# Layer 2 of a twelve-sublayer network on one core: FP4 magnitudes in PSUM, other slots, and kept queue order in the stage before

## The chip, the core and the metric

The kernel runs on one core of a Trainium2 chip (trn2). The metric is the device time of one launch in microseconds (us), lower is better. A core has five engines with a queue each, worked off in the order in which they were built: PE (matrix products and transposes, with its weight loads shown as PEld), DVE (vector), ACT (scalar functions), POOL (GpSimd) and SP (here only DMA issues).

## The reference, cut to what matters

The input is `x` of shape 8 x 512 x 128 in fp32, eight sequences, called batches b here. Twelve sublayers follow each other, each on a layernorm of `x`, each added to `x`. The parts that this case is about:

```python
# layer 1, twice: routed experts with a shared expert (stage l1_ffn), between them 16-head attention (stage l1_attn)
x = x + 0.5 * _L1_ffn_ref(_layernorm(x), ...)
x = x + _L1_attn_ref(_layernorm(x), ...)
x = x + 0.5 * _L1_ffn_ref(_layernorm(x), ...)
# layer 2 and the first sublayer of layer 3 (one stage, layer2)
x = x + 0.5 * _L2_ffn_ref(_layernorm(x), ...)      # FFN with FP4 rounding
x = x + _L2_attn_ref(_layernorm(x), ...)           # gated recurrence along the 512 tokens
x = x + 0.5 * _L2_ffn_ref(_layernorm(x), ...)
x = x + 0.5 * _L3_ffn_ref(_layernorm(x), ...)      # relu FFN
...
def fp4_quant_dequant(x):                          # blocks of 16 along the last axis
    scale = max(max(abs(x)) / 6, 1e-12)
    q = _GRID[searchsorted(_MID, abs(x / scale))] * sign(x) * scale
def _L2_ffn_ref(x, w_gate, w_up, w_down):          # 128 -> 352 -> 128
    h = silu(fp4(x) @ fp4(w_gate).T) * (fp4(x) @ fp4(w_up).T)
    return fp4(h) @ fp4(w_down).T
```

## The kernel before, in words

All eight batches of `x` stay in SBUF for the whole launch. The stages run one after the other: l0_ffn, l0_attn, l0_ffn, l1_ffn, l1_attn, l1_ffn, layer2, l3_attn, l3_ffn. A list scheduler takes the instructions in the order of the program as priorities and pulls an instruction forward where its own clock says that the engine is free and the operands are there; so the order in an engine's queue is not the order of the program. `in_order` (L366) chains the instructions of the named engines that are traced inside its block, so that they keep their order; each block is a chain of its own.

**Stage l1_attn.** For each batch, PE makes scores into PSUM tiles `first` (three banks), DVE takes their row maxima (`max`, L1590, 64 per batch), ACT takes exponentials, PE multiplies with the values. At the end of a batch, `attended` updates `x` on POOL (L1771).

**Stage l1_ffn.** For each batch, `routed(b + 1)` (norm, router, ranks, shares) is emitted in steps between the ten steps of `experts(b)`. An expert is two products (`pg`, `pu`), a silu on ACT (L913), two DVE products (L914, L922) and a product into `po`. In its second run the stage also carries, in the steps (b, 3) and (b, 8), pieces of `layer2_constants`: the decay rate of the recurrence by a chain of small DVE operations (`softplus`), and the FP4 rounding of the three layer-2 weights. The norm in `routed` is `norm` (L322 to L338): eight small DVE instructions, two on POOL, four more on DVE. Before the change no block of this second run is chained, since `aside_at` has an empty set of engines.

**Stage layer2.** Each of the four sublayers is cut into pieces for one batch (or for a pair of batches in the recurrence), each piece has a slot, and all pieces are sorted by slot and emitted in that order. The slot of a piece is that of `_ROUNDED_FFN`, `_RECURRENCE` or `_RELU_FFN`, plus `_STARTS[k]`, plus `_STEPS[k]` times b, with k = 0 for the first FP4 FFN, 1 for the recurrence, 2 for the second FP4 FFN, 3 for the relu FFN.

The pieces of an FP4 FFN for one batch: `stats` and `apply` (norm, the multiplication on ACT), `x_in` and `x_out` (rounding of the normed input), `turned` (transposes on PE, copy on ACT), four `gated` (per 128 tokens: `pg` and `pu` on PE, silu on ACT L1182, product on DVE L1183), `h_in` and `h_out` for two halves (rounding of 704 columns), `h_turned` for two halves (three times two transposes into `ht` L1198 and a copy on ACT L1199), `down` (twelve products into `po`, added to `x` on DVE L431).

Rounding is `fp4_in` (DVE: maximum, scale, reciprocal, L1015 to L1025; then POOL multiplies, L1027) and `fp4_out`: ACT writes `big` = |r| times 2^22 (L1035), DVE passes twice over `big` and `r` (L1036, L1037), POOL multiplies by the scale (L1038). `big` is an SBUF tile with two buffers; `r` lies in SBUF.

PSUM has eight banks in this stage: `mm` two, `pg` two, `pu` two, `ht` one, `po` one.

Of the kernel before, what the change touches and what calls it, by code (L numbers as in the profile page):

```python
# [19 lines left out]
F32 = mybir.dt.float32  # L20
# [6 lines left out]
P = 128  # L27
NB, L, D = 8, 512, 128
NC = L // P
# [173 lines left out]
def _attention_pack(p, wq, bq, wk, bk, wv, bv, wo, bo):  # L203
# [17 lines left out]
    sums=(9, 14, 21, 29),  # L221
    turned=(17, 23, 29, 35),
# [18 lines left out]


_STARTS = (0, 7, 32, 40)
_STEPS = (5.5, 8, 8, 8)
_DOWN = [(0, 128), (128, 128), (256, 96)]
_ROUNDED_FFN = {
    "stats": -9,
    "apply": -5,
    "x_in": -5,
    "x_out": -4,  # L250
    "turned": -1.5,
    "gated": (0.5, 0.5, 1, 1),
    "h_in": (0.5, 2.5),
    "h_out": (2, 4),
    "h_turned": (3.5, 5),
    "down": 7,
}
_RECURRENCE = {
    "stats": -1,
    "apply": 2,  # L260
    "turned": 2,
    "gates": 3.5,
    "decays": 4,
    "exps": 4,
    "roots": 4.5,
    "sums": 5.5,
    "added": 6.5,
}
_RELU_FFN = {
    "stats": 0.5,  # L270
    "apply": 0.5,
    "turned": 2,
    "wide": (3.5, 3.5, 4, 4),
    "product": 5.5,
    "added": 10,
}


class _Kernel:
# [554 lines left out]
    def l1_ffn(self):  # L834


        nc, tc = self.nc, self.tc
        with ExitStack() as s:
            keep = s.enter_context(tc.tile_pool(name="keep", bufs=1))
            self.sb = s.enter_context(tc.tile_pool(name="sb", bufs=2))  # L840
            self.ps = s.enter_context(tc.tile_pool(name="ps", bufs=2, space=bass.MemoryType.PSUM))
            self.shares = keep.tile([P, 8, P], F32R, name="shares")
            nc.vector.tensor_copy(
                self.shares.rearrange("p e m -> p (e m)"), self.w["moe", "spread"]
            )
            self.seqs = [{} for _ in range(NB)]
            for _ in self.routed(0):
                pass
            for b in range(NB):
                ahead = self.routed(b + 1) if b + 1 < NB else iter(())  # L850
                experts = self.experts(b)
                ordered = self.aside_at[0] if b == 1 else ()
                for step in range(10):
                    with self.in_order(*ordered):
                        next(experts)
                        next(ahead, None)
                        if (b, step) in self.aside_at[1]:
                            next(self.aside, None)
                for _ in ahead:
                    pass  # L860
# [166 lines left out]
        nc.gpsimd.tensor_tensor(self.blocks(r), self.blocks(v), self.each(inv), ALU.mult)  # L1027
        return r, scale

    def fp4_out(self, r, scale, sb):  # L1030


        nc = self.nc
        big = sb.tile([P, 2 * 352], F32, name="big")[:, : r.shape[1]]
        nc.scalar.activation(big, r, AF.Abs, scale=2.0**22)  # L1035
        nc.vector.scalar_tensor_tensor(r, big, 1.5 * 2.0**22, r, ALU.max, ALU.add)  # L1036
        nc.vector.scalar_tensor_tensor(r, big, 1.5 * 2.0**22, r, ALU.max, ALU.subtract)  # L1037
        nc.gpsimd.tensor_tensor(self.blocks(r), self.blocks(r), self.each(scale), ALU.mult)  # L1038
# [116 lines left out]
    def rounded_ffn(self, b):  # L1155
        nc = self.nc
        F = 352
        flat = "p c d -> p (c d)"
        wT = self.l2w
        stats, apply, q = self.front(b, "f", 3)  # L1160

        def x_in():
            q["x"] = self.fp4_in(q["xn"].rearrange(flat), self.sb, "x", 3)

        def x_out():
            self.fp4_out(*q["x"], self.sb)

        def turned():
            q["xT"] = self.sb.tile([P, L], F32, name="fxT", bufs=3)
            xq = q["x"][0].rearrange("p (c d) -> p c d", d=D)  # L1170
            self.transposed(xq, self.ps, q["xT"], nc.scalar.copy)

        def gated(c):
            if c % 2 == 0:
                q["h", c // 2] = self.sb.tile([P, 2, F], F32, name="h", bufs=3)
            h = q["h", c // 2][:, c % 2, :]
            tok = q["xT"][:, bass.ts(c, P)]
            pg = self.ps.tile([P, L], F32, name="pg")[:, :F]
            self.mm(pg, tok, wT["w_gate"])
            pu = self.ps.tile([P, L], F32, name="pu")[:, :F]  # L1180
            self.mm(pu, tok, wT["w_up"])
            nc.scalar.activation(h, pg, AF.Silu)  # L1182
            nc.vector.tensor_tensor(h, h, pu, ALU.mult)  # L1183

        def h_in(half):
            q["r", half] = self.fp4_in(q["h", half].rearrange(flat), self.sb, "h", 3)

        def h_out(half):
            self.fp4_out(*q["r", half], self.sb)

        def h_turned(half):
            if half == 0:
                q["hT"] = self.sb.tile([P, 3, L], F32, name="hT", bufs=2)
            hq = q["r", half][0].rearrange("p (j f) -> p j f", f=F)
            for k, (at, n) in enumerate(_DOWN):
                pt = self.ps.tile([P, 2, P], F32, name="ht", bufs=1)
                for j in range(2):
                    nc.tensor.transpose(pt[:n, j, :], hq[:, j, at : at + n], self.ident)  # L1198
                nc.scalar.copy(  # L1199
                    q["hT"][:n, k, bass.ts(half, 2 * P)], pt[:n].rearrange("p c t -> p (c t)")  # L1200
                )

        def down():
            po = self.ps.tile([P, L], F32, name="po", bufs=1)
            for c in range(NC):
                for k, (_, n) in enumerate(_DOWN):
                    self.mm(
                        po[:, bass.ts(c, P)],
                        q["hT"][:n, k, bass.ts(c, P)],
                        wT["w_down"][:n, k, :],  # L1210
                        start=k == 0,
                        stop=k == 2,
                    )
            self.add_half(b, po.rearrange("p (c d) -> p c d", d=D))

        s = _ROUNDED_FFN
        return [
            (s["stats"], stats),
            (s["apply"], apply),
            (s["x_in"], x_in),  # L1220
            (s["x_out"], x_out),
            (s["turned"], turned),
            *((s["gated"][c], partial(gated, c)) for c in range(4)),
            *((s["h_in"][k], partial(h_in, k)) for k in range(2)),
            *((s["h_out"][k], partial(h_out, k)) for k in range(2)),
            *((s["h_turned"][k], partial(h_turned, k)) for k in range(2)),
            (s["down"], down),
        ]

    def recurrence(self, bs):  # L1230
# [7 lines left out]
        sb = self.sb  # L1238
# [10 lines left out]
        def gates():  # L1249
            for k, (_, _, _, q) in enumerate(qs):  # L1250
                for n, bank in (("ig", "pg"), ("ag", "pu")):
                    pg = self.ps.tile([P, L], F32, name=bank)
                    self.mm(pg, a(n + "_w"), q["xT"])
                    q[n] = make(n, k)
                    nc.scalar.activation(q[n], pg, AF.Sigmoid, bias=a(n + "_b"))
# [31 lines left out]
        def added():  # L1287
# [8 lines left out]
            (s["stats"], lambda: all_of(1)),  # L1296
            (s["apply"], lambda: all_of(2)),
            *((s[f.__name__], f) for f in (turned, gates, decays, exps, roots, sums, added)),
        ]

    def relu_ffn(self, b):
        nc = self.nc
        w = lambda n: self.w["l3f", n]
        stats, apply, q = self.front(b, "r", 1)
# [4 lines left out]
            q["h"] = self.sb.tile([P, 4, L], F32, name="rh", bufs=1)  # L1309

        def wide(k):
            ph = self.ps.tile([P, L], F32, name=("pg", "pu")[k % 2])
            self.mm(ph, w("w1")[:, bass.ts(k, P)], q["xT"])
            nc.scalar.activation(q["h"][:, k, :], ph, AF.Relu, bias=w("b1")[:, k : k + 1])

# [7 lines left out]
        def added():  # L1323
# [8 lines left out]
            (s["apply"], apply),  # L1332
            (s["turned"], turned),
            *((s["wide"][k], partial(wide, k)) for k in range(4)),
            (s["product"], product),
            (s["added"], added),
# [468 lines left out]
@with_exitstack  # L1805
def _run_stages(ctx, tc, u, packs, out):
    k = _Kernel(ctx, tc, u, packs, out)
    for at, name in enumerate(_STAGES):
        if at == 3:
            k.aside = k.attention_constants(ctx)  # L1810
            next(k.aside)
            k.aside_at = (mybir.EngineType.Pool, mybir.EngineType.DVE), [(1, n) for n in range(10)]
        if at == 5:
            k.aside = k.layer2_constants(ctx)
            next(k.aside)
            k.aside_at = (), [(b, n) for b in range(NB - 1) for n in (3, 8)]
        getattr(k, name)()
    k.store()

# [17 lines left out]
```

## Time and profile before

| | us |
|---|---|
| median of three runs | 2488.74 (2488.4 to 2490.4) |
| profiled execution, its own time | 2481.17 |
| its span, first to last instruction | 2479.4 |
| stage l1_attn in the trace | about 750 to 1272 |
| second l1_ffn in the trace | about 1272 to 1529 |
| layer2 in the trace | 1529 to 1946 |
| busy in the span: PE, DVE, ACT, POOL | 2147.4, 1657.7, 1235.7, 671.0 |

A row of the timeline is: start, duration, engine, line and operation, output and inputs; in brackets the idle time of that engine just before it, and the instruction of another engine that ended it. A row of the groups is: line, engine, operation, shapes and count; then busy time in us and mean ns of one; then the idle time before and what ended it. A row of the windows is a stretch of the span, its length, and the busy time (and the number of instructions) of each engine in it, then the share of full speed granted to PE, the share of the DMA engines, and GB/s.

### The profile page before, as it was taken

The numbers are of one execution on the slowest core, as the hardware profiler recorded it, in microseconds if no ns is written. First come the engines' busy times: TensorE is split into PE (matmuls) and PEld (weight loads), VectorE is DVE, ScalarE is ACT, GpSimd is POOL, SyncE is SP. The second block draws the span as 40 slices with busy tenths as digits, with TensorE's granted clock in tenths as the row PEclk, the third lists the DMA queues.
The fourth block names the chain that finished last, engine by engine and source line by source line (L and its number), as shares of the span: only waits on it lengthen the run. The fifth ranks groups of instructions, "written<-read, shape, count | busy, mean of one in ns | idle before, by whom it ended". The sixth has DMA issues, their size and how long they took to land.

```text
span 2479.4 us, 30103 instructions
## 1 busy us (share of the span) xinstructions
PE 2147.4 (87%) x10907; PEld 1031.0 (42%) x10967; DVE 1657.7 (67%) x3830; ACT 1235.7 (50%) x1828; POOL 671.0 (27%) x923
## 2 busy tenths in 40 slices
PE   7679998889998989888869997776778899999989
PEld 3444444434444333333324443544444444444444
DVE  4566774568768788888547776879677465666611
ACT  3545663323321667667633333556655235555554
POOL 1123443022111011111121112556555013333330
PEclk9779998989996899999979998878889879999999
DMA  3000000000000000000000000000000000000001
GB/s 118 1 1 1 1 1 13 10 0 1 0 1 0 1 1 1 1 1 1 1 7 1 0 1 0 1 1 1 0 1 1 0 1 1 1 1 1 1 1 34
DMA packets 10036, 13.08 MB, mean 5 GB/s; under 512 B 416, under 2 KB 8736, under 8 KB 9760
## 3 DMA queue, kind: packets, MB, share of 16 engines
q1 hardware_dynamic: 7776, 10.11, 1.2%
q8 instruction: 86, 1.41, 0.2%
q10 hardware_dynamic: 2112, 1.05, 0.2%
q14 instruction: 62, 0.51, 0.1%
HBM read 9.06 MB, written 2.10 MB: 5 GB/s over the span
## 4 chain that ended last, share of the span: by engine, by line
PE 61%; DVE 20%; POOL 9%; ACT 6%; issue 4%; DMA 0%; ACTq 0%; DVEq 0%; SPq 0%; POOLq 0%
PE pair L312 10%; PE av L312 8%; PE first L312 7%; PE po L312 7%; PE mm L312 6%; PE pg L312 5%; PE pu L312 5%; DVE max L1590 4%; ACT e L1698 2%; PE ck L312 2%; PE pr L312 1%; PE pw L312 1%; PE ph L312 1%; PE pi L312 1%; PE pf L312 1%
## 5 line engine op out<-in xcount | busy, mean ns | idle before, releaser
L1590 DVE TENSOR_REDUCE max<-first 128x1 f32<-128x512 f32 (+3 forms) x864 | 534.1, 663 | 189.1 <-PE first L312 165.8
L1698 ACT ACTIVATE e<-pair 128x1024 f32<-128x1024 f32 (+3 forms) x512 | 436.4, 865 | 251.4 <-PE pair L312 239.0
L312 PE MATMUL first<-qkT 32*128 32x512 f32 (+3 forms) x1024 | 341.1, 473 | 40.7 <-DVE max L1590 39.4
L312 PE MATMUL av<-e,v 128*32 128x512 f32 (+3 forms) x2048 | 239.7, 538 | 1.0
L312 PE MATMUL pair<-qkT 32*128 32x512 f32 (+3 forms) x1024 | 223.6, 455 | 19.6 <-ACT e L1698 13.1
L913 ACT ACTIVATE act<-pg 128x512 f32<-128x512 f32 x144 | 86.0, 597 | 233.4 <-PE pg L312 198.4
L312 PEld LDWEIGHTS first<-qkT 32*128 32x128 f32 x1024 | 154.4, 198 | 107.9 <-DVE max L1590 99.1
L312 PE MATMUL pair<-mT,max_rows 32*128 32x512 f32 (+3 forms) x1024 | 192.6, 378 | 1.8 <-DVE mT L1632 1.8
L312 PEld LDWEIGHTS pair<-qkT 32*128 32x128 f32 x1024 | 95.7, 186 | 233.5 <-ACT e L1698 130.8
L1700 POOL TENSOR_SCALAR_AFFINE_SELECT e<-e 128x256 f32<-128x256 f32 x256 | 103.4, 407 | 252.9 <-ACT e L1698 252.5
L312 PE MATMUL po<-act,w_moe 128*128 128x512 f32 x288 | 156.7, 630 | 2.4 <-DVE act L922 2.1
L312 PE MATMUL pg<-xT,w_moe 128*128 128x512 f32 x288 | 153.6, 616 | 0.0
L312 PE MATMUL pu<-xT,w_moe 128*128 128x512 f32 x288 | 148.7, 599 | 0.0
L914 DVE TENSOR_TENSOR act<-act,pu 128x512 f32<-128x512 f32 x144 | 98.2, 682 | 55.7 <-PE pu L312 53.7
L1596 POOL COPY copies<-max 128x128 f32<-128x128 f32 x64 | 22.6, 410 | 337.8 <-DVE max L1590 337.8
L312 PEld LDWEIGHTS pair<-mT,max_rows 32*128 32x128 f32 x1024 | 97.2, 189 | 3.6 <-DVE mT L1632 3.3
L922 DVE TENSOR_TENSOR act<-act,pw 128x512 f32<-128x512 f32 x128 | 87.0, 681 | 15.6 <-PE pw L312 13.8
L951 POOL TENSOR_TENSOR ge<-ge,w_moe 128x64 f32<-128x64 f32 (+1 forms) x32 | 42.8, 1336 | 193.9 <-DVE ge L949 191.0
L1198 PE MATMUL ht<-w_const,h_r 128*128 128x128 f32 (+1 forms) x192 | 47.8, 339 | 53.6 <-POOL h_r L1038 29.4
L1557 ACT CAST qkT<-pair 128x1024 fp32r<-128x1024 f32 x64 | 64.7, 1013 | 41.2 <-PE pair L312 40.7
L312 PEld LDWEIGHTS pu<-xT,w_moe 128*128 128x128 f32 x288 | 53.6, 192 | 63.8 <-issue 59.0
L421 PE MATMUL mm<-w_const,xn 128*128 128x128 f32 x192 | 39.7, 323 | 41.7 <-DVE xn L338 26.0
(398 smaller groups left out, 4299.4 us busy)
## 6 DMA issues: line engine op xcount, KB each, us to landing
w_moe<-in_moe SPq DMA_DIRECT2D x1, 2392.0 KB, 14.2
out<-x SPq DMA_DIRECT2D x8, 256.0 KB, 2.3
x<-in_u ACTq DMA_DIRECT2D x4, 256.0 KB, 6.6
x<-in_u SPq DMA_DIRECT2D x4, 256.0 KB, 6.5
w_mixer<-in_l0a SPq DMA_DIRECT2D x1, 960.5 KB, 8.2
w_mixer<-in_l1a SPq DMA_DIRECT2D x1, 769.0 KB, 4.3
w_ffn<-in_l0f SPq DMA_DIRECT2D x1, 578.0 KB, 7.3
w_ffn<-in_l2f SPq DMA_DIRECT2D x1, 560.0 KB, 3.3
```

Of the source, the lines that this page charges most:

```text
L312: self.nc.tensor.matmul(out, lhsT, rhs, start=start, stop=stop)
L421: self.nc.tensor.transpose(pt[:, c, :], xn[:, c, :], self.ident)
L913: nc.scalar.activation(act, pg, AF.Silu)
L914: nc.vector.tensor_tensor(act, act, pu, ALU.mult)
L922: nc.vector.tensor_tensor(act, act, pw[e % 2], ALU.mult)
L951: nc.gpsimd.tensor_tensor(ge.rearrange(flat), ge.rearrange(flat), self.wide(before, m), ALU.mult)
L1198: nc.tensor.transpose(pt[:n, j, :], hq[:, j, at : at + n], self.ident)
L1557: self.nc.scalar.copy(t, p)
L1590: nc.vector.tensor_reduce(mx[:, c, j, gs[0] : gs[-1] + 1], sc, AX.X, ALU.max, negate=True)
L1596: nc.gpsimd.tensor_copy(copies[:, :, :, :, g], mx[:, :, :, g].unsqueeze(3).to_broadcast([P, NC, 4, 8]),)
L1698: nc.scalar.activation(e[:, :, :n], sc[:, :, :n], AF.Exp, scale=scale)
L1700: nc.gpsimd.affine_select(e[:, :, :P], e[:, :, :P], pattern=[[0, 2], [1, P]], compare_op=ALU.is_ge, fill=0.0, base=0, channel_multiplier=-1,)
```

## The change

It has three parts. `fp4_out` takes a further argument: the calls in layer2 pass 1 and get `big` as a PSUM tile of two banks with one buffer; the calls for the weights keep SBUF, with a tile of their own width. To make room, `pu` goes from two banks to one, and `ht` is gone: its transposes go into the two banks of `mm`. All of layer 2's slots are set anew. And in the second l1_ffn all ten steps of batch 1, and the steps (b, 3) and (b, 8) of the other batches up to 6, are now each chained on POOL and DVE.

```diff
-_STEPS = (5.5, 8, 8, 8)
+_STEPS = (4, 7, 8, 8)
...
-    "stats": -9,
-    "apply": -5,
-    "x_in": -5,
+    "stats": -10,
+    "apply": -6.5,
+    "x_in": -6,
...
-    "h_in": (0.5, 2.5),
-    "h_out": (2, 4),
-    "h_turned": (3.5, 5),
-    "down": 7,
+    "h_in": (0.5, 2),
+    "h_out": (2, 2),
+    "h_turned": (3, 5.5),
+    "down": 6.5,
...
-    "gates": 3.5,
-    "decays": 4,
-    "exps": 4,
-    "roots": 4.5,
-    "sums": 5.5,
-    "added": 6.5,
+    "gates": 4,
+    "decays": 4.5,
+    "exps": 4.5,
+    "roots": 5.5,
+    "sums": 6,
+    "added": 7,
...
-    "wide": (3.5, 3.5, 4, 4),
-    "product": 5.5,
-    "added": 10,
+    "wide": (3.5, 4, 5, 5),
+    "product": 6.5,
+    "added": 9.5,
...
-                ordered = self.aside_at[0] if b == 1 else ()
                 for step in range(10):
+                    ordered = self.aside_at[0] if b == 1 or (b, step) in self.aside_at[1] else ()
...
-    def fp4_out(self, r, scale, sb):
+    def fp4_out(self, r, scale, sb, big=None):
-        big = sb.tile([P, 2 * 352], F32, name="big")[:, : r.shape[1]]
+        n = r.shape[1]
+        if big is None:
+            big = sb.tile([P, n], F32, name="big")
+        else:
+            big = self.ps.tile([P, 2, L], F32, name="big", bufs=1)
+            big = big.rearrange("p k n -> p (k n)")[:, :n]
...
-            self.fp4_out(*q["x"], self.sb)
+            self.fp4_out(*q["x"], self.sb, 1)
...
-            pu = self.ps.tile([P, L], F32, name="pu")[:, :F]
+            pu = self.ps.tile([P, L], F32, name="pu", bufs=1)[:, :F]
...
-            self.fp4_out(*q["r", half], self.sb)
+            self.fp4_out(*q["r", half], self.sb, 1)
...
-                pt = self.ps.tile([P, 2, P], F32, name="ht", bufs=1)
+                pt = self.ps.tile([P, NC, P], F32, name="mm")
...
-                    pg = self.ps.tile([P, L], F32, name=bank)
+                    pg = self.ps.tile([P, L], F32, name=bank, bufs=2 if bank == "pg" else 1)
...
-            ph = self.ps.tile([P, L], F32, name=("pg", "pu")[k % 2])
+            ph = self.ps.tile([P, L], F32, name=("pg", "pu")[k % 2], bufs=2 - k % 2)
...
+    both = mybir.EngineType.Pool, mybir.EngineType.DVE
-            k.aside_at = (), [(b, n) for b in range(NB - 1) for n in (3, 8)]
+            k.aside_at = both, [(b, n) for b in range(NB - 1) for n in (3, 8)]
```

More of the change, by code (lines that the diff above doesn't have):

```diff
@@ L252 @@
     "gated": (0.5, 0.5, 1, 1),
-    "h_in": (0.5, 2.5),
-    "h_out": (2, 4),
-    "h_turned": (3.5, 5),
-    "down": 7,
+    "h_in": (0.5, 2),
+    "h_out": (2, 2),
+    "h_turned": (3, 5.5),
+    "down": 6.5,
 }
 _RECURRENCE = {
-    "stats": -1,
-    "apply": 2,
-    "turned": 2,
-    "gates": 3.5,
-    "decays": 4,
-    "exps": 4,
-    "roots": 4.5,
-    "sums": 5.5,
-    "added": 6.5,
+    "stats": -0.5,
+    "apply": 1.5,
+    "turned": 2.5,
+    "gates": 4,
[4 more added lines that the diff above has]
+    "added": 7,
 }
 _RELU_FFN = {
-    "stats": 0.5,
+    "stats": 0,
     "apply": 0.5,
     "turned": 2,
-    "wide": (3.5, 3.5, 4, 4),
-    "product": 5.5,
-    "added": 10,
+    "wide": (3.5, 4, 5, 5),
+    "product": 6.5,
+    "added": 9.5,
 }
@@ L1199, in h_turned @@
                 nc.scalar.copy(
-                    q["hT"][:n, k, bass.ts(half, 2 * P)], pt[:n].rearrange("p c t -> p (c t)")
+                    q["hT"][:n, k, bass.ts(half, 2 * P)], pt[:n, :2].rearrange("p c t -> p (c t)")
                 )
@@ L1811, in _run_stages @@
             next(k.aside)
-            k.aside_at = (mybir.EngineType.Pool, mybir.EngineType.DVE), [(1, n) for n in range(10)]
+            k.aside_at = both, [(1, n) for n in range(10)]
         if at == 5:
```

## The prediction, made before the changed kernel was run

> **What bounds the kernel now.** I read the page for the shares, the windows for each stage, then the timeline where a stage has gaps.
>
> ```profile
> 1300.00:1526.00 226.00, 224.98 (x621) 96.44 (x619) 161.76 (x378) 73.17 (x113) 30.25 (x35) 1.00 0.00 1
> 1545.00:1857.00 312.00, 224.79 (x911) 143.87 (x912) 246.85 (x570) 184.68 (x368) 185.39 (x157) 0.82 0.00 1
> 1857.00:1946.00 89.00, 70.75 (x274) 40.31 (x273) 50.62 (x145) 45.04 (x90) 35.62 (x34) 0.94 0.00 1
> ```
>
> The second l1_ffn is bound by PE once it runs: 224.98 of 226 us. Layer2 is bound by no engine. In its main stretch DVE is busiest (246.85 of 312 us, 79%), then PE (72%), POOL and ACT (59% each); in-order queues wait for each other. The last 89 us run one batch after another.
>
> In l1_attn, PE and DVE feed each other through the three `first` banks, and four times a norm stands in between that only the next stage needs:
>
> ```profile
> 1073.63 1.98 PE L312 MATMUL pair<-xT,w_mixer 128*128 128x512 f32 x4
> 1074.74 1.27 POOL L1771 TENSOR_TENSOR x<-x,yn 128x512 f32<-128x512 f32 x1
> ...
> 1076.04 0.48 DVE L322 BATCH_NORM_STATS2 xn_st<-x 128x6 f32<-128x128 f32 x2 [2.30 <-POOL x L1771]
> ...
> 1077.05 1.25 DVE L1590 TENSOR_REDUCE max<-first 128x1 f32<-128x512 f32 x2
> 1077.75 0.50 PE L312 MATMUL first<-qkT 32*128 32x512 f32 x1 [1.71 <-DVE max L1590]
> ...
> 1191.53 0.79 PE L312 MATMUL first<-qkT 32*128 32x512 f32 x1 [3.68 <-DVE max L1590]
> ```
>
> The statistics wait 2.30 us for POOL's update of `x`, take 1 us, and hold the maxima behind them on DVE; PE then stands 1.71 us. The same happens at 900, 959, 1018 and 1133, and at 1191 it is 3.68 us.
>
> At the start of the second l1_ffn PE stands for the first batch's shares:
>
> ```profile
> 1274.45 0.15 DVE L821 SCALAR_TENSOR_TENSOR softplus_e<-w_l2a 128x1 f32<-128x1 f32 x1
> ...
> 1277.74 0.21 DVE L966 TENSOR_TENSOR biased<-scores,w_moe 128x64 f32<-128x64 f32 x1
> ...
> 1296.08 1.12 PE L887 MATMUL mm<-w_const,halves 128*128 128x128 f32 x4 [10.34 <-POOL halves L881]
> ```
>
> Between these rows the constants of layer 2 (softplus, weight scales) sit in DVE's queue among the operations of the router.
>
> In layer2, a pass over `big` sometimes takes twice its time:
>
> ```profile
> L1036 DVE SCALAR_TENSOR_TENSOR h_r<-big,h_r 128x704 f32<-128x704 f32 x32 | 33.4, 1043 | 8.2 <-ACT big L1035 8.2
> L1037 DVE SCALAR_TENSOR_TENSOR h_r<-big,h_r 128x704 f32<-128x704 f32 x32 | 32.3, 1010 | 0.1
> ...
> 1869.10 1.39 POOL L1027 TENSOR_TENSOR h_r<-h,h_inv 128x704 f32<-128x704 f32 x1 [0.38 <-DVE h_inv L1025]
> ...
> 1869.58 1.66 DVE L1036 SCALAR_TENSOR_TENSOR h_r<-big,h_r 128x704 f32<-128x704 f32 x1 [0.21 <-ACT big L1035]
> ```
>
> The medians of the two are 892 and 884 ns, the longest 2003 and 1914. In the last two rows the pass that began under a POOL product lasts until 0.75 us after that product's end.
>
> **What the skill says.** "SBUF — State Buffer", Who interferes with whom: a DVE instruction with two SBUF inputs and a GpSimd instruction that reads SBUF exclude each other for a whole instruction; with at most one SBUF input DVE doesn't contend. The rows above agree with the first half; the `add_half` pass with one input in PSUM (L431, 512 columns: median 690 ns, longest 692) fits the second. "PSUM — Partial Sum Buffer", Terms: a bank holds 2 KiB per partition, so 704 fp32 columns need two of eight. "ScalarE: Activation LUTs", What ACT_TABLE_LOAD costs: about 1283 ns a load; the trace has 1283.
>
> **The change part by part**, against the profiled execution's own 2481.17 us.
>
> *Kept order, in l1_attn.* In the built order of the changed kernel the statistics of batches 2 to 5 (at 1018, 1076, 1133, 1190) and the four scalings of batch 2 leave l1_attn for the second l1_ffn, with their POOL steps; batches 0 and 1 stay. PE's waits go: 3 x 1.71 + 3.68 = 8.8 us. The intervals between statistics are 58.3 us with the scalings in them and 56.9 without: 1.4 more. No DMA moves; POOL's reciprocal roots leave a queue with 9 us of work in 57. What is late next is the key/query projection that PE does anyway. Value -10.2 (bounds -7, if later waits take the place, and -15, at DVE's full 3.4 us for each norm).
>
> *Kept order, at the start of l1_ffn.* The softplus chain moves behind batch 0's router, into batch 1's; w_gate's scale goes later still. ACT then loads no exp table ahead of the first scores, which come at 1275.7 instead of 1276.4; `biased` follows at once, 2.0 us earlier. From there to the shares I add the router's pieces with batch 1's durations (1306.24 to 1309.6 for the first part) and the two 1.22 us products, the 2.35 us POOL product, the two 1.22 us reductions and 2.5 us to PE's transposes, with the three expert products (0.68) that the built order puts between: PE's transposes at 1290.3 instead of 1296.08. Value -5.8 (-3 to -7).
>
> *Kept order, within l1_ffn.* DVE gets in batch 1: statistics of five or six batches (1.06 us each, pitch from 1529), scalings of two (1.2 each), a weight's scale and passes (2.3), router 9.6, 17 expert products at 0.62 pitch (10.5), 1.3 for the end: 31 us against PE's 28.6 per batch. Elsewhere (about 25) PE covers it. Value +2.5 (0 to +6); were the cover gone, all 8 us of moved work.
>
> *`big` in PSUM: the lock.* Above its median each pass loses on average 0.151 and 0.126 us (704 columns, x32 each), 0.257 and 0.212 (512 columns, x16): 16.4 us of DVE. POOL's L1027 and L1038 lose against 1.39 and 1.06: 32 x (0.18 + 0.18) + 16 x (0.18 + 0.17) = 17 us. In the chain of waits of this stretch about two thirds of the DVE passes and two fifths of these POOL products lie on the path: 10.5 + 7 = 17.5 at most. The other check: DVE's 247 us less its 14 in the stretch at the same 79% are 17 us. I take -14 (0 to -17.5).
>
> *`big` with one buffer.* The next Abs (0.79 or 0.63 us) can no longer run under the passes before it, and behind a waiting Abs on ACT stand hT copies, silus and norms, for which PE and DVE wait. If nothing fills DVE: 0.79 + 0.63 for each of 16 FFNs, 23 us. The built order has products and maxima of another batch between the passes at first; in the last three batches four h and two x passes follow each other bare. Value +6 (+2 to +23).
>
> *`pu` with one bank.* PE must wait for DVE's product (0.51) of the same 128 tokens; the next `pg` (0.6) covers it unless DVE is late, by some 0.3 us: 48 x 0.3 = 14 us of PE, which is idle 28%. Value +3 (0 to +14).
>
> *Tables.* The built ACT queue has 25 table loads from layer2 on instead of 17, since the gates' sigmoids are split around other functions: 8 x 1.28 = 10.3 us of an engine busy 59%. Value +5 (0 to +10).
>
> *`ht` in two banks.* PE stood 23.9 us for hT copies in layer2 (weight loads 40.7). Value -6 (0 to -20): mostly hidden by down products.
>
> *Slots.* The work is the same; the built order still ends with four batches one after another (21.5 us each before: adds at 1884.6, 1906.5, 1927.9), with one relu FFN more left when the last recurrence ends. I take 0 (-12 to +12), inside the stage's doubt.
>
> Sum: -10.2 - 5.8 + 2.5 - 14 + 6 + 3 + 5 - 6 = -19.5: a profiled execution of 2461.7. The median of runs lies 7.6 us above it; the same difference gives 2488.7 - 19.5 = 2469.
>
> **The rivals.** *Layer2 packs better (2449).* At 81.5% DVE instead of 79 the main stretch needs 233/0.815 = 286 us, -26 instead of -6: another 20. For it: no engine is full. Against: single buffers.
> *The norms only move (2487).* At the weak ends of the bounds: -7 in l1_attn, -3 at the start of l1_ffn, all 8 of the moved work paid in it, and layer2's terms cancel: -2. Against: PE's waits of 1.71 are plain, and DVE has 28% free in l1_ffn.
> *The single `big` decides (2498).* One mechanism: in layer2, ACT's queue stops at each Abs until DVE has done both passes. Priced at a whole Abs, 0.74 us on each of 48 uses, it is 35 instead of 6: -19.5 + 29 = +9.5. It outweighs the rest from 0.53 us per use ((19.5 + 6)/48). For it: h_out of both halves has one slot now; ACT's waits for PE and POOL leave it in step with DVE. Against: the waits of the Abs for DVE were only 4.5 us once, with two buffers.
>
> **How the numbers follow.** Forecast 0.50 (2458 to 2481), packs better 0.20, norms only move 0.12, single `big` 0.18. The range takes half of each neighbour: 2446 to 2496. A measurement of this kernel can tell about 0.2% (5 us). Faster by more than that: 0.50 + 0.20 + 0.04; same: 0.10; slower: 0.16.
>
> **What would show it.** Right: no `xn_st` rows with a wait for L1771 after 960, and l1_attn shorter by about 10; PE's wait for `halves` near 4.5 us instead of 10.3; L1041/L1042 (the passes) with a longest near 0.95 us for 704 columns, and POOL products at 1.39. Wrong: PE gaps over 3 us in l1_ffn's batches 1 and 2; in layer2, Abs rows that wait for a pass for more than 25 us in total, or `pu` rows waiting for `h` for more than 20; a layer2 not shorter than 415 us.

## The result and the profile after

The changed kernel takes 2459.77 us (median of four runs, 2456.21 to 2461.01) against 2489.22 us of the kernel before: 29.45 us less, a ratio of 0.9879 (95% interval 0.9862 to 0.9896). Forecast was 2469. Five further runs gave 2460.04 (ratio 0.9872, 0.9849 to 0.9895). The profiled execution took 2460.62 us, its span is 2458.9.

The stages can be cut at the last `attended` update on POOL, at the last add of `y` in the second l1_ffn and at the last add of layer2 (L431):

| us of the span | before | after |
|---|---|---|
| up to the last attention update | 1276.2 | 1266.4 |
| second l1_ffn | 251.9 | 251.5 |
| layer2 | 418.1 | 407.7 |
| rest | 533.2 | 533.3 |

The two traces differ by 20.5 us, the medians by 29. The table is therefore a first guide only; the section on why the prediction was right returns to the missing 9 us.

The windows of the kernel after, cut where those of before were cut (in l1_ffn, then layer2 up to the last recurrence add, then its end):

```profile
1289.00:1515.00 226.00, 221.52 (x618) 95.61 (x617) 172.16 (x457) 76.80 (x117) 37.17 (x49) 0.99 0.00 1
1535.00:1813.00 278.00, 203.91 (x837) 127.25 (x838) 221.04 (x518) 182.92 (x349) 158.55 (x147) 0.84 0.00 1
1813.00:1926.00 113.00, 89.92 (x344) 49.83 (x342) 64.28 (x193) 54.00 (x112) 41.64 (x44) 0.94 0.00 1
```

Layer2's main stretch is 34 us shorter and its end 24 us longer: more is left over when the last recurrence is done. DVE's work in the two falls from 297.5 to 285.3 us, and its share of the main stretch stays at 79.5% (79.1% before): the stage is not packed better, it has less to do.

PE's waits in l1_attn (window 900 to 1240; columns: total us, times, longest), before and after:

```profile
PE first L312 <- DVE max L1590: 30.4, 53, 3.7
```
```profile
PE first L312 <- DVE max L1595: 20.3, 48, 1.7
```

The longest wait of 3.7 us is gone, and 10.1 us in all. The statistics of the next norm tell why; of the kernel after, their groups and their waits:

```profile
L322 DVE BATCH_NORM_STATS2 xn_st<-x x32: 259/267/295, 900.1 to 1346.4; 128x6 f32<-128x128 f32 x32
...
  POOL x L1776: 4.6, 2
```

They wait for POOL's update of `x` twice, for batches 0 and 1, and not seven times and 18.0 us as before. At the start of l1_ffn, PE's wait for the shares, from the timeline after:

```profile
1283.43 1.11 PE L887 MATMUL mm<-w_const,halves 128*128 128x128 f32 x4 [5.72 <-POOL halves L881]
```

It was 10.34. In layer2, the passes over `big` (ns: shortest, median, longest) and four rows of the timeline after:

```profile
L1041 DVE SCALAR_TENSOR_TENSOR h_r<-big,h_r x32: 822/884/892, 1551.2 to 1900.4; 128x704 f32<-128x704 f32 x32
L1041 DVE SCALAR_TENSOR_TENSOR x_r<-big,x_r x16: 625/682/692, 1529.5 to 1880.5; 128x512 f32<-128x512 f32 x16
```
```profile
1797.07 1.21 DVE L1270 TENSOR_TENSOR_SCAN p<-ag,limit 128x511 f32<-128x511 f32 x1
1797.30 2.16 POOL L1043 TENSOR_TENSOR h_r<-h_r,h_scale 128x704 f32<-128x704 f32 x1 [0.79 <-DVE h_r L1042]
1798.36 0.69 DVE L1041 SCALAR_TENSOR_TENSOR x_r<-big,x_r 128x512 f32<-128x512 f32 x1
1799.08 0.69 DVE L1042 SCALAR_TENSOR_TENSOR x_r<-big,x_r 128x512 f32<-128x512 f32 x1
```

No pass takes more than 892 ns; before, the longest took 2003. In the four rows the POOL product takes 2.16 us, where its median is 1.39, beside the scan, which has both operands in SBUF; the pass over `big` runs in the middle of the same product in its plain 0.69. Above their medians the POOL products of the rounding lost 17.6 us in layer2 before and 3.6 after.

### The profile page after: what moved, and what is told of

Read it like the earlier page. It is cut to its first block, busy times and chain, and to the rows that moved or that the text cites. A ratio compares the mean times of both kernels' runs of the same rounds, so it can differ in the third digit from the quotient of the medians.

```text
span 2458.9 us, 30169 instructions
## 1 busy us (share of the span) xinstructions
PE 2156.8 (88%) x10967; PEld 1025.0 (42%) x10967; DVE 1643.1 (67%) x3830; ACT 1247.7 (51%) x1838; POOL 648.8 (26%) x923
## 4 chain that ended last, share of the span: by engine, by line
PE 60%; DVE 21%; POOL 8%; ACT 7%; issue 4%; DMA 0%; ACTq 0%; DVEq 0%; POOLq 0%; SPq 0%
PE pair L312 11%; PE av L312 8%; PE first L312 7%; PE mm L312 6%; PE po L312 6%; PE pu L312 4%; PE pg L312 4%; DVE max L1595 3%; ACT e L1703 3%; PE ck L312 2%; PE pr L312 2%; PE pw L312 1%; PE ph L312 1%; PE pi L312 1%; PE pf L312 1%
## 5 line engine op out<-in xcount | busy, mean ns | idle before, releaser
L312 PE MATMUL first<-qkT 32*128 32x512 f32 (+3 forms) x1024 | 338.1, 474 | 30.1 <-DVE max L1595 29.4
L312 PEld LDWEIGHTS pg<-xT,w_moe 128*128 128x128 f32 x288 | 52.3, 194 | 54.6 <-issue 54.1
```

The source lines that it names most:

```text
L312: self.nc.tensor.matmul(out, lhsT, rhs, start=start, stop=stop)
```

## The experiments

Each run is compared with runs of the kernel before on the same chip: 2488.52 us for the first four, 2489.73 for the next four, 2485.92 for the last four. All times are medians; a ratio is taken over all runs and is not exactly that of two medians. Where two runs come from different chips, the ratios to the kernel before are the safer comparison.

### The parts by themselves

**Kept order alone.** The kernel before with

```diff
-                ordered = self.aside_at[0] if b == 1 else ()
                 for step in range(10):
+                    ordered = self.aside_at[0] if b == 1 or (b, step) in self.aside_at[1] else ()
...
-            k.aside_at = (), [(b, n) for b in range(NB - 1) for n in (3, 8)]
+            k.aside_at = (mybir.EngineType.Pool, mybir.EngineType.DVE), [(b, n) for b in range(NB - 1) for n in (3, 8)]
```

> The kernel before with the kept order alone (DVE and POOL chained in the steps of the second l1_ffn; slots, big, pu and ht as before). Theory (parts add, each stage keeps its own change): the end of l1_attn comes 9.8 us earlier, l1_ffn is 0.4 us shorter, layer2 unchanged within 2: about -10 us, median 2479. Rival (the order also shifts what layer2 can start on): layer2 changes by more than 3 us, and the sum of the parts fails.

Measured: 2475.77, ratio 0.9944 (0.9932 to 0.9957), -12.8 us. The end of l1_attn lies at 1264.8, 11.4 us earlier than in the trace of before, and l1_ffn takes 251.4. The theory holds in its own stages. Layer2 takes 421.7 in this trace, 3.6 more than in that of before, which is the rival's condition; but the two traces show the same instructions in the same order on PE, DVE, ACT and POOL in layer2, so the 3.6 us are not another order.

**Layer 2 alone.** The changed kernel with the same lines taken back:

```diff
-                    ordered = self.aside_at[0] if b == 1 or (b, step) in self.aside_at[1] else ()
...
+                ordered = self.aside_at[0] if b == 1 else ()
                 for step in range(10):
...
-            k.aside_at = both, [(b, n) for b in range(NB - 1) for n in (3, 8)]
+            k.aside_at = (), [(b, n) for b in range(NB - 1) for n in (3, 8)]
```

> The changed kernel with the kept order taken back (slots, big in PSUM, pu with one bank, ht in mm as changed). Theory: layer2 shorter by the 10.4 us that the two traces show, nothing else: median 2479. Rival (the median moved by 29 where the two traces differ by 20.5, so one of the parts is worth some 9 us more than its trace shows): one of this run and the order alone gives -19, the other -10.

Measured: 2480.13, ratio 0.9963 (0.9948 to 0.9977), -8.4 us, layer2 408.7 in the trace, 9.4 less than before. Both parts are real, and neither alone explains the 9 us by which the medians differ more than the traces.

**PSUM with the old slots.** The previous kernel with `_STEPS` and the three slot tables of before:

```diff
-_STEPS = (4, 7, 8, 8)
+_STEPS = (5.5, 8, 8, 8)
...
-    "h_out": (2, 2),
-    "h_turned": (3, 5.5),
+    "h_out": (2, 4),
+    "h_turned": (3.5, 5),
```

> The kernel before with big in PSUM, pu with one bank and ht in mm, but the old slots and no kept order. Theory of the prediction (slots 0): all of layer2's gain is here, -6 (forecast) to -10, median 2479 to 2483, longest pass 0.9 us. Rival (the new slots make the single buffers bearable): with the old slots Abs waits for the passes and PE for pu, layer2 is not shorter than 418 us, median 2487 to 2500, though the passes are as short.

Measured: 2510.25, ratio 1.0082 (1.0068 to 1.0096): 21.7 us slower than before, though no pass takes more than 893 ns. The prediction's step "slots 0" falls here. The waits of the rival are there (the Abs for the passes 17.3 us, 4.5 before; PE for the product in `pu` 9.9, 5.9 before), but the time lies beyond the rival's 2500 as well.

**The new slots alone.** The kernel before with

```diff
-_STEPS = (5.5, 8, 8, 8)
+_STEPS = (4, 7, 8, 8)
```

and the rest of the slot tables as in the change.

> The kernel before with the new slots alone; big stays in SBUF with two buffers, pu two banks, ht one, no kept order. Theory of the prediction: within 5 us of before (slots 0), and passes that still reach 1.9 us. Rival (the slots are the gain): -8 or more. A third: the slots were set for the single buffers and lose with the old ones, +5 or more.

Measured: 2494.90, ratio 1.0020 (1.0009 to 1.0031), +6.4. The third case of the expectation fits: the slots lose by themselves. So PSUM with its bank moves alone costs 21.7, the slots alone cost 6.4, and both together gain 8.4.

**The changed kernel again**, without an edit.

> The changed kernel once more, unaltered. Theory (the two parts add): order -12.8 and layer 2 -8.4 give -21 us, median 2467. Rival (the two parts help each other, as 2459.8 in the first four runs says): again -27 to -31, median 2458 to 2462. The traces should show where: l1_attn and l1_ffn within 2 us of the order alone, layer2 and what follows carrying the rest.

Measured: 2460.04, ratio 0.9872 (0.9849 to 0.9895). The second case holds by its size. The product of the ratios of the two parts is 0.9944 x 0.9963 = 0.9907, or -23 us; the whole is -29.7. The traces don't show the parts helping each other: in layer2, layer 2 alone and the changed kernel run the same instructions in the same order on all four engines. They show more than the medians of the parts. Layer2 takes 418.1 and 421.7 us with the old slots and banks (before, kept order alone), and 408.7, 407.7 and 405.4 with the new (layer 2 alone, and the changed kernel twice): 12.6 less in the mean. With the 14.5 of the two stages ahead of it (below) that is 27.1 of the 29.7. The intervals of the parts reach to -12.9 and -16.9 us, so the parts may well add; what remains is not shown to be more than spread.

### The memory and the buffers of `big`

**`big` back in SBUF with two buffers**, in the changed kernel:

```diff
-            big = self.ps.tile([P, 2, L], F32, name="big", bufs=1)
-            big = big.rearrange("p k n -> p (k n)")[:, :n]
+            big = sb.tile([P, 2 * 352], F32, name="bigs", bufs=2)[:, :n]
```

> The changed kernel with big put back in SBUF with two buffers; slots, pu with one bank, ht in mm and kept order stay. Theory (the lock is what PSUM buys): passes reach 1.9 us again, the time rises by what the lock costs less the single buffer's cost: 14 - 6 = 8, median 2468. Rival (big in PSUM is worth nothing by itself, the two buffers give back what the lock takes): within 4 us of the changed kernel. Rival (the lock is worth its whole 14 or more, the single buffer nothing under the new slots): 2474 or more.

Measured: 2486.99, ratio 0.9989 (0.9979 to 1.0000): 27 us slower than the changed kernel, more than the first theory and in the range of the last case.

**The same with one buffer** (`bufs=1` in the line above).

> The changed kernel with big in SBUF with ONE buffer, all else as changed: against the changed kernel only the memory differs, against the run with two buffers only the buffer. Theory: lock 14, so 2474; 6 above the run with two buffers. Rival (a single buffer costs nothing under the new slots): equal to the run with two buffers within 3 us.

Measured: 2480.93, ratio 0.9962 (0.9948 to 0.9975), 21 us slower than the changed kernel and 6 faster than with two buffers. That fewer buffers are faster can't be the buffers' doing. In both, the order of DVE's queue in layer2 differs from that of the changed kernel: the list scheduler had answered to the edit. These two runs mix the edit with another order, so both were taken again without that.

**One buffer, the queues held.** The same edit, and at the end of the program every engine's instructions are chained in the built order of the changed kernel (the edges of `in_order`, from a list of the instructions); the built queues are then the same one by one.

> The changed kernel with big in SBUF with one buffer, and every engine's queue held, instruction by instruction, to the built order of the changed kernel; so against the changed kernel nothing but the memory of big differs (in the run before it the scheduler also rearranged the queues). Theory (what big in SBUF lost there is the lock between DVE and POOL): +15 to +22, median 2475 to 2482, passes of up to 1.9 us. Rival (most of that loss was the other order): +8 or less, median at most 2468, though the passes are as long.

Measured: 2480.01, ratio 0.9971 (0.9960 to 0.9982). The median is 20 us above that of the changed kernel, but from another chip; by the ratios (0.9971 against 0.9872 and 0.9879) it is 23 to 25. Nothing but the memory of `big` and the added edges differs, and in the traces all four engines run the same instructions in the same order in layer2. No run holds the queues with `big` in PSUM; but up to layer2, where the queues are held too, this trace takes 1518.4 us, and that of the changed kernel 1517.9. Layer2 takes 421.5 us in the trace, 15 more than the 407.7 and 405.4 of the changed kernel's two. The longest passes take 1887 and 1811 ns again (704 and 512 columns). The groups in layer2 (after the first bar busy us and mean ns):

```profile
L1027 POOL TENSOR_TENSOR h_r<-h,h_inv 128x704 f32<-128x704 f32 x32 | 47.5, 1483 | 29.6 <-DVE h_inv L1025 22.4 <-PE pu L312 3.0 <-PE mm L1202 2.4
...
L1040 DVE SCALAR_TENSOR_TENSOR h_r<-bigs,h_r 128x704 f32<-128x704 f32 x32 | 31.2, 974 | 13.9 <-ACT bigs L1039 13.7
...
L1040 DVE SCALAR_TENSOR_TENSOR x_r<-bigs,x_r 128x512 f32<-128x512 f32 x16 | 17.7, 1107 | 3.5 <-ACT bigs L1039 3.4
```

The means of the changed kernel are 1397, 879 and 676. With the second pass, the lengthening is 11.8 us on DVE, and 4.7 on POOL in L1027: 16.5 us of work, about as much as the 15 that the stage grows by. How much of it lies on the path wasn't measured.

**Two buffers, the queues held** (`bufs=2`, all else as in the run before).

> As the run before it (queues held to the built order of the changed kernel, big in SBUF), with two buffers for big. The order being the same, the difference of the two is the wait of the next Abs for the passes, alone. Theory of the prediction (6 us, 2 to 23): 6 faster than with one buffer. Rival (under this order the single buffer costs nothing): equal within 3.

Measured: 2478.78, ratio 0.9970 (0.9960 to 0.9981), 1.2 us less than with one buffer, inside the spread; layer2 takes 421.5 us in both traces. The rival holds. The waits say why, with one buffer and then with two:

```profile
PE mm L1202 <- POOL h_r L1042: 30.4, 14, 6.3
...
ACT hT L1203 <- PE mm L1202: 26.6, 30, 3.8
...
ACT bigs L1039 <- DVE h_r L1041: 10.6, 10, 2.9
```
```profile
ACT hT L1203 <- PE mm L1202: 37.3, 33, 4.9
...
PE mm L1202 <- POOL h_r L1042: 30.5, 14, 6.3
```

The Abs waits 10.6 us for the passes with one buffer and not at all with two, but ACT then spends the same 10.7 us more in front of PE's transposes. PE, at the end of that chain, waits 30.4 and 30.5. The wait has moved along an engine that is early anyway.

### The banks that were given up, with the old slots

**One buffer for `big`, in SBUF**, in the kernel before (for the weights' rounding too, which shares the line):

```diff
-        big = sb.tile([P, 2 * 352], F32, name="big")[:, : r.shape[1]]
+        big = sb.tile([P, 2 * 352], F32, name="big", bufs=1)[:, : r.shape[1]]
```

> The kernel before with one buffer for big instead of two, still in SBUF, old slots, no kept order. Theory (with the old slots the single buffer is what made big in PSUM 22 us slower): +22 plus what the lock no longer gives back, 20 to 36 us, median 2508 to 2524. Rival (the loss came from pu with one bank or ht in mm): within 5 us of before, median 2484 to 2494.

Measured: 2493.71, ratio 1.0011 (0.9996 to 1.0027), +4.0, with no change still inside the interval. The theory falls: the single buffer isn't what cost 22 us with the old slots.

**`ht` into `mm`**, in the kernel before:

```diff
-                pt = self.ps.tile([P, 2, P], F32, name="ht", bufs=1)
+                pt = self.ps.tile([P, NC, P], F32, name="mm")
```

> The kernel before with ht gone: its transposes go into the two banks of mm; all else as before (old slots, big in SBUF, pu two banks). big in PSUM with the old slots was 22 us slower than before although one buffer for big alone costs some 4 and its lock is gone. Theory (the banks given up cost it, and it is ht in mm, since mm then serves the transposes of x, of h and the sums): +15 to +35, median 2504 to 2524. Rival (pu): within 5 of before. The prediction had -6 for this step.

Measured: 2509.14, ratio 1.0093 (1.0076 to 1.0110), +23.2, in the theory's range. PE's timeline in the kernel before, and in this one, at about the same point of layer2, each with POOL's last product on the `x_r` that PE then transposes:

```profile
1569.01 1.64 POOL L1038 TENSOR_TENSOR x_r<-x_r,x_scale 128x512 f32<-128x512 f32 x1 [0.63 <-DVE x_r L1037]
...
1570.74 0.66 PE L1198 MATMUL ht<-w_const,h_r 128*96 128x128 f32 x2
1571.20 0.64 PE L312 MATMUL po<-w_downT,hT 128*128 128x128 f32 x2
1571.62 0.85 PE L421 MATMUL mm<-w_const,x_r 128*128 128x128 f32 x3
1572.26 1.92 PE L312 MATMUL po<-w_downT,hT 96*128 96x128 f32 x8
```
```profile
1575.62 1.05 POOL L1038 TENSOR_TENSOR x_r<-x_r,x_scale 128x512 f32<-128x512 f32 x1
...
1589.52 1.82 PE L1198 MATMUL mm<-w_const,h_r 128*128 128x128 f32 x6 [5.63 <-POOL h_r L1038]
1591.13 0.64 PE L312 MATMUL po<-w_downT,hT 128*128 128x128 f32 x2
1591.56 1.06 PE L421 MATMUL mm<-w_const,x_r 128*128 128x128 f32 x4
...
1608.44 1.11 PE L1198 MATMUL mm<-w_const,h_r 128*128 128x128 f32 x4 [5.77 <-POOL h_r L1038]
...
1611.33 1.06 PE L421 MATMUL mm<-w_const,x_r 128*128 128x128 f32 x4
```

In the first, the transposes of the next batch's `x_r` begin 1.0 us after it is ready, between products of `po`. In the second, it is ready at 1576.7 and its transposes begin at 1591.6: they stand behind the transposes of `h_r`, which wait 5.6 us for POOL (5.8 for the batch after). From the end of POOL's product to the first transpose, added over the sixteen `x_r`, it is 23.0 us before, 118.6 in this run, 126.7 with everything in PSUM and the old slots, and 26.1 in the changed kernel. The slots give the reason: with the old ones `turned` of batch b+1 has slot -1.5 + 5.5 = 4, after the 3.5 of the first `h_turned` of batch b. Two pieces that take the same two banks take them in the order of emission, so the next batch can't start its products before this batch's `h` is rounded. With a step of 4 it is -1.5 + 4 = 2.5, ahead of `h_turned` at 3. PE's own waits for `h_r` in layer2 are 29.4, 75.0, 60.4 and 24.0 us in the same four. They are the weaker sign: with the new slots alone they are 51.0, while the `x_r` stand for 13.9 in all.

**One bank for `pu`**, in the kernel before:

```diff
-            pu = self.ps.tile([P, L], F32, name="pu")[:, :F]
+            pu = self.ps.tile([P, L], F32, name="pu", bufs=1)[:, :F]
```

with the same bank count in the two other places that use `pu`.

> The kernel before with one bank for pu instead of two; all else as before. Theory (ht in mm is what cost): within 5 us of before; the prediction had +3 (0 to 14). Rival (PE's wait for the product of the same 128 tokens is what cost with the old slots): +15 to +35.

Measured: 2506.53, ratio 1.0074 (1.0060 to 1.0087), +20.6. Both expectations took it that one of the two banks was to blame; each costs by itself. With the single buffer's 4.0, and less the 15 to 20 us of the lock, their sum is 28 to 33 us, and PSUM with the old slots measured 21.7: the parts don't simply add, and what the lock is worth under the old slots wasn't measured. PE's own waits for the product (8.4 us, before 5.9) don't explain it; weight loads wait 19.0 (before 10.2). The built ACT queue changes: table loads in layer2 of this run, of which the kernel before has four for each of four lines, 16 in all:

```profile
L1255 ACT ACT_TABLE_LOAD x8 | 10.3, 1283 | 0.1
...
L1276 ACT ACT_TABLE_LOAD x5 | 6.4, 1283 | 0.1
...
L1261 ACT ACT_TABLE_LOAD x4 | 5.1, 1283 | 0.1
L1271 ACT ACT_TABLE_LOAD x4 | 5.1, 1283 | 0.1
L1182 ACT ACT_TABLE_LOAD x4 | 5.1, 1283 | 0.1
...
L1272 ACT ACT_TABLE_LOAD x1 | 1.3, 1283 | 0.0
```

26 loads, ten more: 12.8 us of ACT. With `ht` in `mm` alone there are 16, with one buffer for `big` or with the new slots alone 18. So most of the loads come with the single bank of `pu`; how much of the 20.6 us is theirs wasn't separated.

In none of these three runs were the queues held, and in all three the order of DVE's, ACT's and POOL's queues in layer2 is another than before. What they measure is the bank or buffer together with the scheduler's answer to it. For `ht` in `mm` the standing transposes show a direct cost; for `pu` the share of the bank itself is open.

### Where layer2 gains and loses

Times after the last add of l1_ffn, read from the adds in each trace:

| kernel | last recurrence add | last add of layer2 | between |
|---|---|---|---|
| before | 328.5 | 418.1 | 89.6 |
| new slots alone | 311.2 | 424.1 | 113.0 |
| PSUM, old slots | 347.3 | 437.6 | 90.2 |
| `ht` in `mm` | 348.4 | 440.9 | 92.5 |
| `pu` one bank | 346.5 | 440.6 | 94.0 |
| layer 2 alone | 296.2 | 408.7 | 112.5 |
| changed | 295.4 | 407.7 | 112.3 |

The banks given up make the main stretch 18 to 20 us longer under the old slots. The new slots make it 17 shorter, or 51 shorter where the banks are short (PSUM with the old slots against layer 2 alone), and leave 22 to 23 more for the end.

## Why the prediction was right, and where its steps failed

**Kept order, in l1_attn: -10.2.** Right. Seven traces without the kept order and seven with it can be compared. From the first to the last attention update they take 378.9 us in the mean without and 367.2 with it: -11.7. PE's waits for the maxima fall by 10.1 between the two traces shown. One reading was off: after the statistics at 959 PE does not stand in the trace of before; the 1.71 comes at 900, 1018, 1076 and 1133. The sum takes only batches 2 to 5, and is right.

**Start of l1_ffn and its batch 1: -5.8 + 2.5.** Right in sum. From the last attention update to the first add of l1_ffn it is 52.4 without and 49.0 with (-3.4), from there to the last add 202.0 and 202.6 (+0.6). The start gained 3.4 of the 5.8 (PE's wait for the shares fell from 10.34 to 5.72, not to the 4.5 that was named), and the later cost of 2.5 did not come: 0.6. The two misses cancel.

**The frame.** The sum was made against before's profiled execution, and its 7.6 us to the median were taken as constant. They weren't: that execution reached the end of l1_ffn at 1528.1, the seven traces without the kept order at 1528.1 to 1539.8, 1534.3 in the mean, with the same instructions in the same order up to there (but for a few in the run with one buffer for `big`). The seven with it lie at 1513.0 to 1521.1, 1517.8 in the mean. So 6 of the 9 us by which the medians differ more than the traces were in the trace of before, which was an early one; the rest isn't placed.

**The lock: -14 (0 to -17.5).** The mechanism right, and the size: 15 us in the stage with identical queues; the whole kernel says more, 20 by the medians and 23 to 25 by the ratios. The Trainium skill ("SBUF — State Buffer", Who interferes with whom) says that only a DVE instruction with two SBUF inputs, or one in a two-port mode, shuts out a POOL instruction that reads SBUF; the passes with `big` in PSUM, which still write SBUF, agree (0.69 us under a running product).

**`big` with one buffer: +6 (2 to 23).** Wrong: 1.2 with the order held, and +4 under the old slots with the order not held, both inside the spread. The term took a wait of ACT for a loss of the stage. The wait exists (7.9 us in the changed kernel) and, where the order was held, is taken from another wait of ACT. With it falls the rival "single `big` decides", which priced this wait at 35.

**`pu` one bank +3, `ht` in two banks -6, slots 0.** Here the argument failed, and by luck the errors nearly cancelled. Under the old slots the two bank moves cost 20.6 and 23.2 (with the scheduler's answer), and the slots are worth 6.4 of loss with the old banks and 30 of gain with the new ones (2510.25 to 2480.13). The prediction priced each by its direct waits and treated the order of emission as fixed. What `ht` in `mm` does is to tie two pieces of different batches to each other, and what the slots do is to turn that order round. Sharing two banks was booked as a gain of 6 because `ht` got a second one; that the other user of these banks might stand behind it was missed.

**Tables +5.** The changed kernel has 24 loads in layer2, eight more than before, as the built order said; the run with one bank for `pu` shows which edit brings most of them. What they cost in time wasn't measured.

**Sum.** In layer2 the forecast was -6; layer 2 alone gave -8.4 by the medians, and 12.6 less by the traces. The kept order was put at -13.5; alone it gave -12.8, and 14.5 by the traces. The lock and the kept order were forecast with their mechanisms. That the rest of layer2 came to little is luck: it holds two bank moves that cost by themselves, and slots that take this back.

## What to carry to other kernels

Price a PSUM bank that is shared anew by who else takes it, and in which order the two are emitted: the wait that it brings is not in the profile of before. When an edit changes a buffer, hold the built order of the queues and measure again, because the scheduler's answer to the edit can be larger than the edit's own effect: the two runs with two buffers for `big`, on two chips, differ by some 5 us by their ratios (0.9989 and 0.9970) and by 11 in layer2 of their traces (432.8 and 421.5), while the buffer itself makes 1.2. A wait that an engine gains counts only if the next engine in the chain then waits longer.

## What was not expected of the hardware

The Abs that writes 704 columns takes 762 ns in the mean into PSUM and 790 into SBUF, for 512 columns 596 and 626: some 30 ns less at both widths. And a DVE instruction with a single SBUF operand can be held up too. In the changed kernel the scaling L411 (128 columns, normally 0.34 us) stands against three POOL products in a row, the third of which (1.26 us, from 1792.97) isn't shown:

```profile
1790.23 4.09 DVE L411 TENSOR_SCALAR xn<-x,xn_mv,xn_rstd 128x128 f32<-128x128 f32 x3
1790.29 1.38 POOL L1043 TENSOR_TENSOR h_r<-h_r,h_scale 128x704 f32<-128x704 f32 x1 [2.45 <-DVE h_r L1042]
...
1791.63 1.39 POOL L1027 TENSOR_TENSOR h_r<-h,h_inv 128x704 f32<-128x704 f32 x1
```

Three scalings take 4.09 us where they would take 1.0. The longest in layer2 was 739 ns before and is 1522 now. This fits the two-port case of the same section of the Trainium skill, which names `tensor_scalar`, and which the prediction's reading of it left out; that these scalings run in such a mode no run here shows. `big` has left the lock, these haven't.
